# Four scan sweeps of a convolution layer: VectorE kept in the text's order, and the statistics of a column block taken eight steps behind its sum

## The chip, the cores and the metric

The kernel runs on one core of a Trainium2 chip. The metric is the device time of one execution in microseconds; a kernel's time is the median of its runs.

## What is computed

The input is an image of 48 channels and 128 x 128 pixels in fp32. Four layers follow one another. Each normalises its input in groups of channels, passes it through a block and adds the result to the input:

```
x = x + attention(_gn(x))       # layer 0
x = x + sweeps(_gn(x))          # layer 1
x = x + patch convolution(_gn(x))   # layer 2
x = x + state space scan(_gn(x))    # layer 3
```

`_gn` subtracts the mean of a group of three channels over the whole image and divides by its standard deviation. So a layer can't begin to normalise before the last pixel of the layer ahead of it is summed and counted.

The layer of this case is layer 1. It goes over the image line by line, and each line is its input plus a convolution (five taps, 48 channels to 48, with a bias) of the line before:

```
def step(w, b):
    def f(carry, inp):
        nxt = inp + _conv1d(carry, w, b)
        return (nxt, nxt)
    return f
```

There are four such sweeps, each over the result of the one before: down the rows, up the rows, to the right over the columns, and to the left over the columns. Every step needs the result of the step before it.

## The kernel before

`tile_kernel` calls `attention`, `sweeps`, `patch_conv`, `image_out` and `scan` in turn. Two large buffers in SBUF, `xa` and `xb`, each 128 partitions high, hold the image. In `sweeps` (L553 to L688) `other` is `xb` and `xq` is `xa`. The rows of the image lie in `t`, a view of `xb`, for the first two sweeps, and its columns in `u`, a view of `xa`, for the last two.

`steps` (L618 to L626) lists 508 steps, 127 for each sweep; step n computes one line. `down`, `up` and `right` (L627) are 127, 254 and 381 and mark the ends of the first, second and third sweep. So the left sweep begins at n = 381, and step n of it computes column 507 - n.

One step of the loop (L654) is this. Three matmuls (L656) on TensorE add the convolution of the line before into the PSUM tile `p`, which `begin` (L632) has already started with the input line and the bias. `begin` for the next step is written behind them. Then VectorE multiplies `p` with `mask` into the new line (L664). That line is the operand of the next step's matmuls, so the matmuls and the multiply follow one another in a ring. While the up sweep runs, `turn` copies its rows into columns on ScalarE (L640).

While the left sweep runs, the residual sum is made as well. `sums` (L643 to L645) divides the columns into blocks: seven of 16 columns, then 8, 4 and 4 at the end. At the step that computes a block's leftmost column (n = 395 for x = 112, and then every 16 steps up to n = 491 for x = 16, and 499, 503 and 507 for x = 8, 4 and 0), GpSimd adds the block of `u` to the layer's input, which has been loaded into `xb` (L672, L677). Each block is then cut into pieces of 512 elements, four for a block of 16 columns, two for the block of 8 and one for each of the last two, and put into the list `todo` (L683). `stretch` (L648) takes a piece from the list and runs `bn_stats` on it on VectorE (L650), which leaves its mean and variance in `st`. There are 32 pieces. The text calls `stretch` at every third step if more than four pieces wait (L684), and for the rest after the loop (L687).

At the beginning of the next layer, `group_stats` (L71) puts the 32 results together, and the layer's normalisation (L93) waits for it. The borders that this layer sets on GpSimd (L747, L760) and its loads of weights (L103, L105, L713 and the following lines) are written after the sweeps in the text.

The order of the instructions on each engine is not that of the text. The kernel is written in a tile framework, whose scheduler orders the instructions of an engine by its own estimate of when each can begin, and sets the semaphores. Where the order is to be kept, the kernel uses the class `InOrder` (L38 to L60). It stands in for an engine and ties each instruction that it issues to the one issued before it, so that the scheduler can't exchange the two; the tie sets no semaphore. `attend`, for example, issues through it on ScalarE and TensorE (L310). In `sweeps` VectorE's instructions are not tied.

Of the kernel before, what the change touches and what calls it, by code (L numbers as in the profile page):

```python
# [27 lines left out]
H = W = 128  # L28
# [37 lines left out]
def group_stats(nc, pool, psum, const, name="gn_ps"):  # L66


    st, gmat = const["st"], const["gmat"]
    mv = pool.tile([C, 2], F32, name="gn_mv")  # L70
    nc.vector.bn_aggr(mv, st)  # L71
    pm = psum.tile([C, 1], F32, name=name)
    nc.tensor.matmul(pm, lhsT=gmat, rhs=mv[:, 0:1], start=True, stop=True)
    mean = pool.tile([C, 1], F32, name="gn_mean")
    nc.vector.tensor_copy(mean, pm)

    dev = pool.tile([C, 1], F32, name="gn_dev")
    nc.vector.tensor_sub(dev, mv[:, 0:1], mean)
    var = pool.tile([C, 1], F32, name="gn_var")
    nc.vector.scalar_tensor_tensor(var, dev, dev, mv[:, 1:2], ALU.mult, ALU.add)  # L80
    pv = psum.tile([C, 1], F32, name=name)
    nc.tensor.matmul(pv, lhsT=gmat, rhs=var, start=True, stop=True)
    std = pool.tile([C, 1], F32, name="gn_std")
    nc.vector.tensor_scalar_add(std, pv, 1e-5)  # L84
    nc.scalar.activation(std, std, AF.Sqrt)  # L85
    rstd = pool.tile([C, 1], F32, name="gn_rstd")
    nc.vector.reciprocal(rstd, std)
    return mean, rstd
# [7 lines left out]
def rows(ap, n=W):  # L96
    return ap.rearrange("c (r w) -> c r w", w=n)
# [455 lines left out]
@with_exitstack  # L553
def sweeps(ctx, tc, xq, other, x1, const, ins):

    nc = tc.nc
    pool = ctx.enter_context(tc.tile_pool(name="l1", bufs=1))
    ps1 = ctx.enter_context(tc.tile_pool(name="l1_ps1", bufs=1, space=PSUM))
    ps = ctx.enter_context(tc.tile_pool(name="l1_ps", bufs=2, space=PSUM))
    K = 64 + C
    E = 3
    S = W + 2 * E
    L = W + 1


    w = pool.tile([128, 3, 3, K], F32, name="w")
    nc.sync.dma_start(w, ins["l1_w"])
    wi = pool.tile([128, 3, K], F32, name="wi")
    nc.sync.dma_start(wi, ins["l1_wi"])
    mask = pool.tile([128, L], F32, name="mask")
    nc.gpsimd.memset(mask, 1.0)
    nc.gpsimd.memset(mask[0:C, 0:1], 0.0)
    nc.gpsimd.memset(mask[64:128, W : W + 1], 0.0)


    t = other[:, 0 : S * S].rearrange("c (h s) -> c h s", s=S)
    u = xq[:, 0 : W * S].rearrange("c (w s) -> c w s", s=S)
    low, high = slice(0, E - 1), slice(S - E, S)

    def borders(b, lines):

        inside = slice(E - 1, E + W)
        nc.gpsimd.memset(b[32:64, lines, inside], 1.0)
        for pad in (low, high):  # L590
            nc.gpsimd.memset(b[:, lines, pad], 0.0)
        nc.gpsimd.memset(b[0:C, lines, E - 1 : E], 0.0)
        nc.gpsimd.memset(b[64:K, lines, E + W - 1 : E + W], 0.0)  # L593

    borders(t, slice(E, E + H))
    mean, rstd = group_stats(nc, pool, ps1, const)
    off = pool.tile([C, 1], F32, name="off")
    nc.vector.scalar_tensor_tensor(off, mean, -1.0, rstd, ALU.mult, ALU.mult)
    RN = 8
    for r in range(0, H, RN):  # L600
        for at, x in ((0, E), (64, E - 1)):
            nc.scalar.activation(
                t[at : at + C, E + r : E + r + RN, x : x + W],
                rows(xq[0:C, r * W : (r + RN) * W]),
                AF.Identity,
                bias=off,
                scale=rstd,
            )

    borders(u, slice(0, W))  # L610

    def row(h):
        return t[:, E + h, :]

    def col(x):
        return u[:, x, :]

    steps = []  # L618
    for h in range(1, H):
        steps.append((0, row(h), row(h), row(h - 1)))  # L620
    for h in range(H - 2, -1, -1):
        steps.append((0, row(h), row((h - 1) % H), row(h + 1)))
    for x in range(1, W):
        steps.append((1, col(x), col(x), col(x - 1)))
    for x in range(W - 2, -1, -1):
        steps.append((2, col(x), col(x), col(x + 1)))  # L626
    down, up, right = H - 1, 2 * (H - 1), 3 * (H - 1)  # L627

    def begin(n):
        which, _, inp, _ = steps[n]  # L630
        p = ps.tile([K, L], F32, name="p")
        nc.tensor.matmul(  # L632
            p, lhsT=wi[0:K, which, :], rhs=inp[0:K, E - 1 : E + W], start=True, stop=False
        )
        return p

    def turn(h):

        for at, y in ((0, E + h), (64, E + h - 1)):
            nc.scalar.copy(u[at : at + C, :, y], t[0:C, E + h, E : E + W])  # L640


    sums = {}  # L643
    for x, width in [(x, 16) for x in range(16, W, 16)] + [(8, 8), (4, 4), (0, 4)]:
        sums[x] = rows(other[0:C, 0:N])[:, :, x : x + width]  # L645
    todo, done = [], []

    def stretch():  # L648
        xr = todo.pop(0)
        nc.vector.bn_stats(const["st"][:, len(done), :], xr)  # L650
        done.append(xr)

    p = begin(0)
    for n, (which, out, inp, state) in enumerate(steps):  # L654
        for i in range(3):
            nc.tensor.matmul(  # L656
                p,
                lhsT=w[0:K, which, i, :],
                rhs=state[0:K, 2 * i : 2 * i + L],
                start=False,  # L660
                stop=(i == 2),
            )
        nxt = begin(n + 1) if n + 1 < len(steps) and n + 1 != up else None
        nc.vector.tensor_mul(out[0:K, E - 1 : E + W], p, mask[0:K])  # L664
        if n == down:
            turn(H - 1)
        if down <= n < up:
            turn(H - 2 - (n - down))
        if n + 1 == up:

            for r in range(0, N, 2048):
                nc.sync.dma_start(other[0:C, r : r + 2048], x1[:, r : r + 2048])  # L672
            nxt = begin(up)
        x = 4 * (H - 1) - 1 - n
        if n >= right and x in sums:
            xr = sums[x]
            nc.gpsimd.tensor_add(  # L677
                xr,
                xr,
                u[0:C, x : x + xr.shape[2], E : E + H].rearrange("c w h -> c h w"),  # L680
            )
            step = CH // xr.shape[2]
            todo += [xr[:, r : r + step] for r in range(0, H, step)]  # L683
        if n % 3 == 0 and len(todo) > 4:  # L684
            stretch()
        p = nxt
    while todo:  # L687
        stretch()  # L688
# [800 lines left out]
@with_exitstack  # L1489
def tile_kernel(ctx: ExitStack, tc: tile.TileContext, ins: dict, out: bass.AP):  # L1490
    nc = tc.nc
    cp = ctx.enter_context(tc.tile_pool(name="const", bufs=1))
    dram = ctx.enter_context(tc.tile_pool(name="x3", bufs=1, space=bass.MemoryType.DRAM))
    const = constants_on_chip(tc, cp, ins)
    x1 = dram.tile([C, N], F32, name="x1")
    x3 = dram.tile([C, N], F32, name="x3")
    with ExitStack() as image:
        xp = image.enter_context(tc.tile_pool(name="image", bufs=1))

        xa = xp.tile([128, W * (W + 6)], F32, name="xa")  # L1500
        xb = xp.tile([128, (H + 6) * (W + 6)], F32, name="xb")
        for i in range(0, N, 2048):
            nc.sync.dma_start(xa[0:C, i : i + 2048], ins["x"][:, i : i + 2048])
        attention(tc, xa, xb, x1, const, ins)
        sweeps(tc, xa, xb, x1, const, ins)
        patch_conv(tc, xb, xa, const, ins)
        image_out(tc, xb, x3, const)
    scan(tc, x3, const, ins, out)
# [189 lines left out]
```

## Time and profile before

| | |
|---|---|
| time before, median of 3 runs | 7754.8 us (7753.7 to 7766.08) |
| profiled execution, span | 7757.9 us |
| PE, ACT, DVE and POOL busy | 81%, 57%, 44%, 36% of the span |
| L664, the multiply of a step | 508, 291 to 295 ns each for most |
| L650, statistics of a piece | 32, 676 ns each |
| L677, GpSimd's sum, seven of 48 x 2048 | 5.5 us each |
| L677, one of 48 x 1024 and two of 48 x 512 | 2.81 us, 1.48 and 1.50 us |
| first and last multiply of the rows' two sweeps | 3844.1 and 4177.4 us |
| first and last multiply of the columns' two sweeps | 4180.8 and 4565.1 us |

PE is TensorE, DVE is VectorE, ACT is ScalarE and POOL is GpSimd. All starts are microseconds from the span's start. A line of the timeline gives the start, the duration, the engine, the line of the kernel, the operation, what is written and read, and in brackets how long the engine was idle before it and whose result ended that. "x6" says that six instructions are merged in one line. PEclk is the clock that TensorE was granted, as a share of the full one. Each fp32 matmul of the text is carried out as several instructions, so TensorE's counts are larger than those of the text.

### The profile page before, as it was taken

What the parts mean: (1) busy time and instruction counts of PE and PEld (TensorE: products, weight loads), DVE (VectorE), ACT (ScalarE), POOL (GpSimd) and SP (SyncE); (2) the same over time, 40 slices, a digit from 0 to 9 for tenths busy, and PEclk for the clock granted to TensorE, in tenths of its full rate; (3) what the DMA queues carried; (4) which work ended last, traced back from release to release, by engine and by line L of the source; (5) the groups of instructions that cost most, each with busy time, mean ns of one, the idle gap of its engine ahead of it and who ended that gap; (6) DMA issues with size and microseconds to landing.
All of it is one profiled execution on the core that took longest, in us unless ns stands there. A gap on an engine that the chain in (4) does not pass through costs nothing. (4 is left out here: it accounts for less than half of the span.)

```text
span 7757.9 us, 203399 instructions
## 1 busy us (share of the span) xinstructions
PE 6262.9 (81%) x93872; PEld 3179.6 (41%) x93872; DVE 3376.3 (44%) x2467; ACT 4458.0 (57%) x4928; POOL 2793.1 (36%) x573
## 2 busy tenths in 40 slices
PE   7999999999999999999888879845545554554555
PEld 2333333333333333333377655434334343434444
DVE  8300000000000000000122224489999999999998
ACT  2566666666666666666623014366666666666665
POOL 1000000000000000000100112279999999999998
PEclk9999999999999999999999989866766766776666
DMA  5000000000000000000000001156556566666776
GB/s 75 11 2 3 3 2 3 3 3 2 3 3 3 2 3 3 3 2 3 6 5 13 1 27 50 25 150 166 158 160 164 151 162 156 165 156 159 182 179 148
DMA packets 167598, 488.84 MB, mean 63 GB/s; under 512 B 33441, under 2 KB 51969, under 8 KB 163985
## 3 DMA queue, kind: packets, MB, share of 16 engines
q1 hardware_dynamic: 160704, 470.30, 24.2%
q8 instruction: 737, 12.08, 0.7%
q10 hardware_dynamic: 6032, 5.44, 0.3%
q14 instruction: 125, 1.02, 0.0%
HBM read 428.86 MB, written 22.02 MB: 58 GB/s over the span
## 5 line engine op out<-in xcount | busy, mean ns | idle before, releaser
L48 ACT ACTIVATE e<-s,absT 128x1024 f32<-128x1024 f32 x2048 | 2279.3, 1115 | 1215.1 <-PE s L48 1215.1
L1458 POOL TENSOR_TENSOR h<-du,bt 128x3072 f32<-128x3072 f32 (+1 forms) x386 | 2559.8, 6681 | 100.9 <-DMA du<-rep 73.0
L48 PE MATMUL s<-xa,xb 49*64 49x512 f32 x16384 | 2124.3, 589 | 10.6 <-DVE xb L266 10.6
L48 PE MATMUL acc<-e,xb 64*64 64x512 f32 x16384 | 2120.3, 588 | 0.0
L1465 DVE TENSOR_TENSOR_SCAN h<-dA,carry,h 128x1024 f32<-128x1024 f32 x864 | 1940.1, 2323 | 48.1 <-ACT dA L48 31.9
L48 ACT ACTIVATE dA<-dt,a 128x1024 f32<-128x1024 f32 x1152 | 1287.2, 1118 | 866.5 <-DVE h L1465 855.6
L48 PE MATMUL y<-h,cw 128*32 128x48 f32 x49152 | 908.6, 247 | 950.5 <-issue 504.4
L361 DVE TENSOR_TENSOR osum<-o 128x512 f32<-128x512 f32 x32 | 22.1, 692 | 3114.0 <-ACT o L48 3114.0
L593 POOL MEMSET xa<- 48x128 f32 x1 | 0.3, 328 | 3560.2 <-PE acc L48 3560.2
L48 PEld LDWEIGHTS y<-h,cw 128*32 128x32 f32 x49152 | 818.3, 141 | 1072.3 <-issue 656.6
L48 PEld LDWEIGHTS s<-xa,xb 49*64 49x64 f32 x16384 | 618.1, 132 | 1158.8 <-issue 607.2
L48 PEld LDWEIGHTS acc<-e,xb 64*64 64x64 f32 x16384 | 620.4, 132 | 1141.6 <-issue 1118.9
L1465 DVE TENSOR_TENSOR_SCAN h<-dA,h 128x1024 f32<-128x1024 f32 x288 | 636.1, 2270 | 45.6 <-ACT dA L48 34.8
L48 PE MATMUL yz<-ev,sel 128*8 128x48 f32 x4096 | 193.0, 259 | 273.0 <-ACT ev L48 270.2
L656 PE MATMUL p<-xa,w 112*112 112x129 f32 x1524 | 258.4, 310 | 66.4 <-DVE xa L664 66.1
L48 PEld LDWEIGHTS yz<-ev,sel 128*8 128x8 f32 x4096 | 162.5, 106 | 331.1 <-ACT ev L48 301.2
L656 PE MATMUL p<-xb,w 112*112 112x129 f32 x1524 | 236.5, 291 | 41.8 <-DVE xb L664 41.7
L677 POOL TENSOR_TENSOR xb<-xb,xa 48x2048 f32<-48x2048 f32 (+2 forms) x10 | 44.3, 4430 | 618.8 <-DVE xa L664 618.8
L656 PEld LDWEIGHTS p<-xa,w 112*112 112x112 f32 x1524 | 202.6, 194 | 120.4 <-DVE xa L664 120.4
L85 ACT ACTIVATE gn_std<-gn_std 48x1 f32<-48x1 f32 x4 | 0.8, 203 | 425.3 <-DVE gn_std L84 419.0
L656 PEld LDWEIGHTS p<-xb,w 112*112 112x112 f32 x1524 | 184.3, 179 | 93.7 <-DVE xb L664 93.7
L640 ACT COPY xa<-xb 48x128 f32<-48x128 f32 x256 | 107.4, 420 | 197.2 <-issue 138.8
(187 smaller groups left out, 3719.3 us busy)
## 6 DMA issues: line engine op xcount, KB each, us to landing
du<-rep SPq DMA_DIRECT2D x768, 256.0 KB
dt<-rep SPq DMA_DIRECT2D x768, 256.0 KB
rest<-xa SPq DMA_DIRECT2D x96, 77.0 KB
rest<-band SPq DMA_DIRECT2D x48, 129.9 KB
rep<-dd SPq DMA_DIRECT2D x24, 192.0 KB
yd<-ys ACTq DMA_DIRECT2D x256, 12.0 KB
band<-band SPq DMA_DIRECT2D x8, 414.4 KB
xa<-xa SPq DMA_DIRECT2D x16, 199.1 KB
```

What stands on the lines that cost most here:

```text
L48: ins = method(*args, **kwargs).ins
L85: nc.scalar.activation(std, std, AF.Sqrt)
L361: nc.vector.tensor_add(self.o, o[:, 0], o[:, 1])
L593: nc.gpsimd.memset(b[64:K, lines, E + W - 1 : E + W], 0.0)
L640: nc.scalar.copy(u[at : at + C, :, y], t[0:C, E + h, E : E + W])
L656: nc.tensor.matmul(p, lhsT=w[0:K, which, i, :], rhs=state[0:K, 2 * i : 2 * i + L], start=False, stop=(i == 2),)
L677: nc.gpsimd.tensor_add(xr, xr, u[0:C, x : x + xr.shape[2], E : E + H].rearrange("c w h -> c h w"),)
L1458: nc.gpsimd.tensor_mul(h[:, p, ks], du.unsqueeze(1).to_broadcast([128, ks.stop - ks.start, LC]), r["bt"][:, ks],)
L1465: nc.vector.tensor_tensor_scan(h[:, p, k, :], dA, h[:, p, k, :], carry[:, i, k : k + 1] if ci else 0.0, ALU.mult, ALU.add,)
```

## The change

VectorE's instructions of the sweeps, that is the multiplies and the statistics, are issued through an `InOrder`, so that they keep the order of the text. A piece enters the list with the step from which it may be taken, eight after the step that issued the sum of its block. A step takes one piece, if the first of the list is due, and does so behind its multiply; the rule of every third step with more than four waiting is gone. What is left after the loop is taken there, as before. The statistics of a piece keep their places in `st`.

```diff
     todo, done = [], []
+    dve = InOrder(tc, nc.vector)
 
     def stretch():
-        xr = todo.pop(0)
-        nc.vector.bn_stats(const["st"][:, len(done), :], xr)
+        _, xr = todo.pop(0)
+        dve.bn_stats(const["st"][:, len(done), :], xr)
         done.append(xr)
...
-        nc.vector.tensor_mul(out[0:K, E - 1 : E + W], p, mask[0:K])
+        dve.tensor_mul(out[0:K, E - 1 : E + W], p, mask[0:K])
...
             step = CH // xr.shape[2]
-            todo += [xr[:, r : r + step] for r in range(0, H, step)]
-        if n % 3 == 0 and len(todo) > 4:
+            todo += [(n + 8, xr[:, r : r + step]) for r in range(0, H, step)]
+        if todo and n >= todo[0][0]:
             stretch()
```

## The prediction

> **What bounds the kernel now.** I read the page first: PE 81%, ACT 57%, DVE 44% and POOL 36% busy over the span, so nothing is full everywhere and the answer lies in a stage. The chain that ended last names only the final stage (L1465, L1458) and does not reach back to the sweeps, so I went to the busy times by stretch of time, of the end of the third sweep and of the stretch in which the sums and their statistics are made:
>
> ```profile
> core 0: us, PE busy (x) PEld busy (x) DVE busy (x) ACT busy (x) POOL busy (x), PEclk, DMA share, GB/s
> 4180.00:4365.00 185.00, 161.68 (x1134) 132.69 (x1134) 41.59 (x142) 0.00 (x0) 0.04 (x1) 0.99 0.01 2
> 4365.00:4565.00 200.00, 156.89 (x894) 131.70 (x894) 50.87 (x142) 0.00 (x0) 57.00 (x25) 0.81 0.00 1
> ```
>
> Both stretches run the same loop. The first has 142 VectorE instructions in 185 us and a TensorE clock of 0.99; the second has 142 in 200 us, but 31 of those are statistics, so fewer steps got done, at a clock of 0.81. The waits by source line, between 4364 and 4566 us, say on whom VectorE waits (busy us and mean ns; then idle before):
>
> ```profile
> L664 DVE TENSOR_TENSOR xa<-p,mask 112x129 f32<-112x129 f32 x113 | 32.9, 291 | 116.4 <-PE p L656 116.4
> L650 DVE BATCH_NORM_STATS2 st<-xb 48x6 f32<-48x512 f32 x31 | 20.4, 676 | 34.0 <-POOL xb L677 34.0
> ```
>
> The second line is the point: VectorE stands idle 34.0 us for GpSimd's sum (L677) in front of L650. The timeline shows one such place (start, duration, then the idle time before and its releaser):
>
> ```profile
> 4364.96 5.49 POOL L677 TENSOR_TENSOR xb<-xb,xa 48x2048 f32<-48x2048 f32 x1 [475.87 <-DVE xa L664]
> 4365.83 0.29 DVE L664 TENSOR_TENSOR xa<-p,mask 112x129 f32<-112x129 f32 x1 [1.01 <-PE p L656]
> 4366.18 0.92 PE L656 MATMUL p<-xa,w 112*112 112x129 f32 x6 [0.17 <-DVE xa L664]
> ...
> 4370.49 0.69 DVE L650 BATCH_NORM_STATS2 st<-xb 48x6 f32<-48x512 f32 x1 [4.36 <-POOL xb L677]
> ...
> 4371.10 0.27 DVE L664 TENSOR_TENSOR xa<-p,mask 112x129 f32<-112x129 f32 x1
> 4371.29 1.27 DVE L650 BATCH_NORM_STATS2 st<-xb 48x6 f32<-48x512 f32 x2
> ...
> 4371.42 1.63 PE L656 MATMUL p<-xa,w 112*112 112x129 f32 x6 [4.10 <-DVE xa L664]
> ```
>
> A step is a closed ring: three products on TensorE, the multiply L664 on VectorE, and TensorE again. One step takes 1.299 us (138 steps between the multiplies at 4185.27 and 4364.53 us). At 4367.1 the matmuls are done and the next multiply could go; but VectorE's queue has a statistics instruction ahead of it, which starts only at 4370.49, when the sum is over. So the multiply comes at 4371.10, 5.27 us after the last. In the program's text this L650 stands at n = 411 at the earliest, fourteen steps later (L684 asks for more than four waiting pieces, and a block brings four): the framework's scheduler has pulled it forward. And TensorE, idle 4.10 us, then takes 1.63 us for the burst that took 0.92. The stretch ends on this ring; what follows (L71, then the next layer) needs the last statistics, and so inherits every microsecond.
>
> [...] full clock for the 138 steps, whose TensorE gaps are below 0.4 us; after the 4.10 us gap come steps of about 2.01 us. [...] L664 reads one operand from PSUM; the multiply at 4365.83, inside a sum, took 0.29 like all others. [...]
>
> **The change part by part.**
>
> *Statistics no longer ahead of the multiplies.* I split the loss from the sum of block x=112 (multiply n=395, at 4364.53) to the last multiply (n=507, at 4565.13): 112 steps in 200.60 us. At 1.299 they would take 145.5; the loss is 55.1 us. Direct waits: the nine intervals between multiplies that hold a wait are 5.27, 5.29, 5.29, 5.30, 5.28, 5.28, 5.29 (the seven wide blocks), 3.19 (x=8) and 2.58 (x=4). Less 1.30 each, that is 27.9 + 1.9 + 1.3 = 31.1 us. The rest, 24.0 us, are 34 slow steps behind these waits at about 2.01 instead of 1.30 (34 x 0.71 = 24.1). The two agree with the total.
>
> *Is the sum there eight steps later?* Eight steps are 10.4 us. A sum starts 0.43 us after its multiply's start and takes 5.5, so it is over at 5.9 us: 4.5 us to spare. Blocks are sixteen steps apart (20.8 us) and their four pieces leave at steps 8 to 11, so nothing piles up. The nearest case, x=16 (n=491, pieces at 499 to 502) before x=8 (n=499, due 507), also fits. GpSimd's other work there is the border memsets of the next layer (L760, 0.94 us each), pulled into its idle time; those on columns still to be added stand behind the sum anyway, and two take 1.83 us, within the margin. So all direct waits go, and with them the gaps that slow the clock: minus 55.1 us.
>
> *One statistics instruction inside a step.* It now follows the multiply. In the trace such a one starts 0.19 us after the multiply's start (4371.29 after 4371.10) and ends about 0.88 after it; the next multiply is due at 1.30. It fits with 0.42 us to spare in VectorE's idle 1.01 us. The step from 4373.09 to 4375.10, with one inside, took 2.01, like slow steps without. It also overlaps no sum except at the end. I cost it at 0; the upper bound, all 29 statistics inside the loop at their full 0.68, is 19.7 us, the lower 0, as it only adds work.
>
> *The end.* Now three pieces (the second of x=8, x=4, x=0) and the one that falls at n=507 follow the last multiply. Four at 0.60 us apart (4371.29, 1.27 us for two) from 0.20 us on: the last starts at 2.0 us. Before, it waited for the last sum and started at 1.88 (4567.01 less 4565.13). Plus 0.1 us, between 0 and 0.6.
>
> *Not moved:* instruction counts, DMAs and their queues (SP's x1 loads L672 ran in the second sweep), GpSimd's sums, and the first 395 steps. The setup loads of the next layer are issued at 4565.45, right behind the last multiply, so they move forward with it. The next layer fills TensorE (100.00 of 100 us busy from 4700 to 4900) and the last is held by VectorE and GpSimd (98.30 and 100.00 of 100 in 5100 to 5200): both run just as long, earlier. One small unknown is the clock at entry: 14 matmuls at 4576.11 took 6.40 us, 12 at 4600.78 took 3.18. If warm, they would save up to 2.7 us, but the matmuls behind them, which read copies issued from 4574.38 on, start only at 4586.90; I take 0.
>
> Sum: -55.1 + 0.1 = **-55.0 us**. On the profiled execution's span of 7757.9 that is 7702.9; the three runs lie at 7753.7 to 7766.08, and off their median of 7754.8 it gives **7699.8 us**.
>
> **The rivals.**
>
> *The statistics don't hide in the step.* For it: VectorE has one more instruction per step, on its critical ring. Against: 0.42 us of slack. Time: 7699.8 + 19.7 = 7719.5. Chance 0.05.
>
> *The change doesn't do what it says, or gives the gain back later:* the scheduler puts the statistics elsewhere, or the next layer waits for something that doesn't move. For it: the scheduler already overruled the text. Against: the order is tied instruction to instruction, and the next layer's loads hang on the last multiply. Time: 7755. Chance 0.04.
>
> *Slower: the clock falls and stays down.* Mechanism: with statistics between the multiplies the TensorE gaps grow and the half clock, today on 34 of 112 steps, holds for nearly all. At 2.015 instead of 1.299, all 112 cost 80.2 us, against 55.1 of loss today: 25 us slower, 7780. It decides from 55.1 / 0.716 = 77 slow steps on. For it: slow runs after one wait lasted up to six steps without more waits. Against: 138 steps in a row at 0.99 with the same gaps. Chance 0.03.
>
> **How the numbers follow.** Forecast 0.88, rivals 0.05, 0.04, 0.03. The range reaches down to 7690 (the warm entry, 2.7, the lowest run, 1.1 below the median[...]) and up to 7720 (the statistics not hidden; the highest of the three runs, 11.3 above the median, lies within). A measurement can tell about 0.2%, 15.5 us, from no change. Forecast and first rival are faster: 0.93; same 0.04; slower 0.03.
>
> **What would show it.** In the changed profile: no idle time of DVE L650 for POOL L677 except at most at the last; multiplies 1.30 us apart from x=112 to the end, 29 of the 32 statistics each right behind a multiply; clock near 1.0 in place of 0.81; the last multiply 145.5 us after n=395; next layer as long as before. Wrong if steps with statistics are longer than 1.30, if slow steps stay without waits, or if the next layer starts 55 us earlier and ends less so.

## The result, and the profile after

The changed kernel takes 7700.5 us (median of 4 runs, 7695.29 to 7707.8); the kernel before, run beside it, takes 7756.2 (4 runs). The ratio is 0.9927, with a 95% interval of 0.9909 to 0.9944: 0.7% faster, and clear of the 0.2% that a measurement can tell. The forecast was 7699.8.

The busy times by stretch of time, of the changed kernel, show the right sweep with the first steps of the left one, and then the time of the sums (columns as before):

```profile
4180.00:4365.00 185.00, 161.36 (x1129) 132.85 (x1130) 41.02 (x140) 0.39 (x1) 0.00 (x0) 0.99 0.01 3
4365.00:4512.00 147.00, 128.32 (x906) 105.14 (x904) 49.67 (x141) 0.00 (x0) 57.34 (x25) 1.00 0.00 1
```

The second stretch now takes 147 us for nearly the VectorE work (141 instructions, 49.67 us) that took 200 us before, and its clock is 1.00 instead of 0.81. GpSimd's work in it, 57.34 us, is nearly the same (57.00).

The groups of instructions between 4364 and 4520 us show who waits. The statistics and the multiplies now have the line of the helper, L48, so they are told apart by their tiles:

```profile
L678 POOL TENSOR_TENSOR xb<-xb,xa 48x2048 f32<-48x2048 f32 (+2 forms) x10 | 44.6, 4464 | 563.0 <-DVE xa L48 563.0
L48 DVE TENSOR_TENSOR xa<-p,mask 112x129 f32<-112x129 f32 x115 | 33.7, 293 | 99.2 <-PE p L657 99.2
L48 DVE BATCH_NORM_STATS2 st<-xb 48x6 f32<-48x512 f32 x32 | 21.4, 675 | 0.0
```

In the last line stands 0.0 where 34.0 us of waiting for GpSimd stood. The timeline shows the first block, whose multiply n = 395 began at 4366.46 (start, duration, and in brackets the idle time before):

```profile
4366.88 5.54 POOL L678 TENSOR_TENSOR xb<-xb,xa 48x2048 f32<-48x2048 f32 x1 [475.40 <-DVE xa L48]
...
4376.86 0.29 DVE L48 TENSOR_TENSOR xa<-p,mask 112x129 f32<-112x129 f32 x1 [1.01 <-PE p L657]
4377.06 0.68 DVE L48 BATCH_NORM_STATS2 st<-xb 48x6 f32<-48x512 f32 x1
4377.20 0.92 PE L657 MATMUL p<-xa,w 112*112 112x129 f32 x6 [0.16 <-DVE xa L48]
4378.15 0.29 DVE L48 TENSOR_TENSOR xa<-p,mask 112x129 f32<-112x129 f32 x1 [0.41 <-PE p L657]
4378.36 0.68 DVE L48 BATCH_NORM_STATS2 st<-xb 48x6 f32<-48x512 f32 x1
```

The sum is over at 4372.42. Its first piece is taken at 4377.06, 4.6 us later, with no wait in front of it. The next multiply comes 1.29 us after the last, and VectorE even then idles 0.41 us for TensorE instead of 1.01: the statistics lie inside the idle time. The burst stays at 0.92 us. From n = 395 to the last multiply (4512.01) it is 145.55 us, and every step in between takes 1.30. This stretch is called "the stretch" below; it was 200.60 us in the kernel before.

At the end of the sweep four statistics follow the last multiply, one of them taken at the last step:

```profile
4512.01 0.29 DVE L48 TENSOR_TENSOR xa<-p,mask 112x129 f32<-112x129 f32 x1 [1.01 <-PE p L657]
4512.22 2.45 DVE L48 BATCH_NORM_STATS2 st<-xb 48x6 f32<-48x512 f32 x4
...
4512.38 1.50 POOL L678 TENSOR_TENSOR xb<-xb,xa 48x512 f32<-48x512 f32 x1 [3.62 <-DVE xa L48]
...
4514.70 1.01 DVE L71 BATCH_NORM_AGGREGATE gn_mv<-st 48x2 f32<-48x192 f32 x1
```

L71 begins 2.69 us after the last multiply, against 2.60 (4567.73 less 4565.13) before.

Of the profiled spans, 7757.9 and 7706.0, the difference is 51.9 us: the stretch gave 55.05, the end took 0.09, the multiply n = 395 came 1.93 later in this execution, and from L71 to the end it took 1.1 more. The last two lie in parts that the change doesn't touch.

### The profile page after: what moved, and what is told of

It is laid out like the page before. It is cut to its first block, busy times and chain, and to the rows that moved or that the text cites. A ratio compares the mean times of both kernels' runs of the same rounds, so it can differ in the third digit from the quotient of the medians.

```text
span 7706.0 us, 203399 instructions
## 1 busy us (share of the span) xinstructions
PE 6227.8 (81%) x93872; PEld 3159.4 (41%) x93872; DVE 3377.0 (44%) x2467; ACT 4455.4 (58%) x4928; POOL 2793.0 (36%) x573
## 5 line engine op out<-in xcount | busy, mean ns | idle before, releaser
L48 ACT ACTIVATE e<-s,absT 128x1024 f32<-128x1024 f32 x2048 | 2277.3, 1114 | 1217.9 <-PE s L48 1217.9
L48 PE MATMUL s<-xa,xb 49*64 49x512 f32 x16384 | 2128.4, 589 | 10.6 <-DVE xb L266 10.6
L48 PE MATMUL acc<-e,xb 64*64 64x512 f32 x16384 | 2125.0, 588 | 0.0
L48 ACT ACTIVATE dA<-dt,a 128x1024 f32<-128x1024 f32 x1152 | 1287.2, 1118 | 864.0 <-DVE h L1466 854.5
L48 PE MATMUL y<-h,cw 128*32 128x48 f32 x49152 | 899.2, 246 | 949.0 <-issue 511.9
L48 PEld LDWEIGHTS y<-h,cw 128*32 128x32 f32 x49152 | 809.9, 140 | 1072.3 <-issue 661.8
L48 PEld LDWEIGHTS s<-xa,xb 49*64 49x64 f32 x16384 | 626.3, 132 | 1151.2 <-issue 615.6
L48 PEld LDWEIGHTS acc<-e,xb 64*64 64x64 f32 x16384 | 628.6, 132 | 1133.7 <-issue 1111.2
L48 PE MATMUL yz<-ev,sel 128*8 128x48 f32 x4096 | 192.9, 260 | 277.2 <-ACT ev L48 273.3
L48 PEld LDWEIGHTS yz<-ev,sel 128*8 128x8 f32 x4096 | 162.5, 106 | 334.9 <-ACT ev L48 308.7
L657 PE MATMUL p<-xa,w 112*112 112x129 f32 x1524 | 233.5, 289 | 41.8 <-DVE xa L48 41.8
L678 POOL TENSOR_TENSOR xb<-xb,xa 48x2048 f32<-48x2048 f32 (+2 forms) x10 | 44.6, 4464 | 563.0 <-DVE xa L48 563.0
L657 PEld LDWEIGHTS p<-xa,w 112*112 112x112 f32 x1524 | 181.8, 177 | 93.3 <-DVE xa L48 93.3
L369 DVE RECIPROCAL rec<-y 48x512 f32<-48x512 f32 x32 | 107.1, 3348 | 257.5 <-ACT y L48 257.5
```

Source lines behind the costliest of these rows:

```text
L48: ins = method(*args, **kwargs).ins
L369: nc.vector.reciprocal(rec, y[64 : 64 + C])
L657: nc.tensor.matmul(p, lhsT=w[0:K, which, i, :], rhs=state[0:K, 2 * i : 2 * i + L], start=False, stop=(i == 2),)
L678: nc.gpsimd.tensor_add(xr, xr, u[0:C, x : x + xr.shape[2], E : E + H].rearrange("c w h -> c h w"),)
```

## The experiments

The stretch is read off the profile of each kernel, as the time from the multiply of n = 395 to the last one. "Median" is the time of the whole kernel; those with one run are marked. A single run's time also holds differences from other parts of the kernel: with four steps, layer 3 alone took 8.6 us longer than in the profile of the changed kernel. So the stretch is what to compare.

| kernel | median, us | kernel before beside it | stretch, us |
|---|---|---|---|
| before | | 7756.2 | 200.60 |
| changed | 7700.5 | 7756.2 | 145.55 |
| tie alone, old rule | 7704.1 | 7752.2 | 145.52 |
| eight-step rule alone | 7755.1 | 7752.2 | 201.44 |
| one step behind the sum | 7749.0 | 7752.2 | 199.34 |
| two steps | 7738.5 (one run) | 7758.6 | 182.76 |
| three steps | 7723.9 (one run) | 7758.6 | 167.44 |
| three steps, again | 7720.6 (one run) | 7756.8 | 159.17 |
| four steps | 7717.8 (one run) | 7758.6 | 146.22 |
| all statistics after the loop | 7715.6 | 7752.2 | 145.52 |
| each statistics twice | 7717.1 (one run) | 7756.8 | 151.40 |
| each three times | 7752.8 (one run) | 7758.6 | 191.71 |

### Which of the two parts does it

The tie alone, with the old rule:

```diff
-        if todo and n >= todo[0][0]:
+        if n % 3 == 0 and len(todo) > 4:
             stretch()
```

> VectorE is tied to the text's order, but the old rule decides when a piece is taken (every third step with more than four waiting), so the first piece of a block comes sixteen steps behind its sum. Theory (the order is what counts, and any distance over 5.9 us will do): no wait of a statistics instruction for GpSimd's sum inside the loop, 145.5 us from the multiply of n = 395 to the last one, clock near 1.0, seven statistics left behind the last multiply instead of four, 1.8 us more at the end; so 53 us below the kernel before. Rival (the eight-step rule is needed, or statistics that now overlap a sum get in its way): waits or longer steps stay, and less than 45 us are gained.

Measured: a stretch of 145.52 us, a ratio to the kernel before of 0.9935 (0.9918 to 0.9952). L71 begins 4.48 us after the last multiply instead of 2.69, so the seven statistics left over cost 1.8 us more, as expected. The statistics that now run beside a sum got in nobody's way: one at 4385.18 took 0.68 us, and the sum that began under it at 4385.41 took 5.55.

The eight-step rule alone:

```diff
-    dve = InOrder(tc, nc.vector)
+    dve = nc.vector
```

> The eight-step rule without the tie: the scheduler may move the statistics. Theory: it pulls them forward as before, the same nine waits stand, 200.6 us from the multiply of n = 395 to the last, same time as before within 0.2%. Rival (the place in the text decides): 145.5 us there, and 55 us below the kernel before.

Measured: a stretch of 201.44 us and a ratio of 1.0002 (0.9993 to 1.0011). The timeline of this kernel shows the first statistics again ahead of the multiply of n = 397 (the third line), although the text puts it behind that of n = 403:

```profile
4361.40 0.29 DVE L665 TENSOR_TENSOR xa<-p,mask 112x129 f32<-112x129 f32 x1 [1.01 <-PE p L657]
4366.06 0.69 DVE L651 BATCH_NORM_STATS2 st<-xb 48x6 f32<-48x512 f32 x1 [4.37 <-POOL xb L678]
4366.67 0.27 DVE L665 TENSOR_TENSOR xa<-p,mask 112x129 f32<-112x129 f32 x1
4366.86 1.27 DVE L651 BATCH_NORM_STATS2 st<-xb 48x6 f32<-48x512 f32 x2
```

So the tie carries the gain. The rule of eight steps alone does nothing, since the scheduler overrules it; under the tie it is worth the 1.8 us at the end.

### Is it the wait for the sum

The tie kept, the distance cut from eight steps to one, two, three and four:

```diff
-            todo += [(n + 8, xr[:, r : r + step]) for r in range(0, H, step)]
+            todo += [(n + 1, xr[:, r : r + step]) for r in range(0, H, step)]
```

> The tie kept, but a piece may be taken one step behind its sum. Theory (the wait for the sum is the cost, whoever puts the instruction there): the first piece of each wide block again waits until 5.9 us after the sum's multiply, so seven intervals of 5.3 us, the clock falls again behind each; 195 to 203 us from n = 395 to the last multiply, same time as before within 8 us. Rival (the tie itself, or one piece per step, is the gain): 145.5 us, 55 us below before.

> A piece may be taken two steps behind its sum. The first piece of a wide block then stands behind the multiply at 2.60 us and waits until about 5.96; the next multiply comes at 6.57 instead of 3.90. Theory (direct wait and clock are two costs): 7 x 2.67 = 18.7 us of direct waits, and a TensorE gap of 3.0 us. If a gap of that length leaves the clock alone, 164.2 us from n = 395 to the last multiply; if it lowers it as the gap of 4.1 us did, some 24 us more, 188. Rival (all of the loss scales with the wait): 55.1 x 18.7 / 31.1 = 33 us of loss, 178.6 us.

> Three steps behind the sum: the first piece stands behind the multiply at 3.90 us, the next multiply comes at 6.57 instead of 5.20, so 7 x 1.37 = 9.6 us of direct waits and TensorE gaps of 1.7 us. Theory (a short gap leaves the clock alone): no slow steps, 155.1 us from n = 395 to the last multiply. Rival (all of the loss scales with the wait): 17 us of loss, 162.5 us.

> Four steps behind the sum: the first piece waits about 0.5 us, but has a slack of 0.42 in its step, so 7 x 0.1 us at most are lost. Theory: 145.5 to 146.3 us from n = 395 to the last multiply, the whole gain. Rival (eight steps are needed): several us more.

With one step the loss is back, tie or no tie: 199.34 us, the ratio 0.9994 (0.9985 to 1.0003). The groups between 4355 and 4566 us of this kernel:

```profile
L48 DVE BATCH_NORM_STATS2 st<-xb 48x6 f32<-48x512 f32 x32 | 21.7, 678 | 34.4 <-POOL xb L678 34.4
```

34.4 us of waiting before the 32 statistics, against 35.6 before the 32 of the kernel before (34.0 for the 31 that ran up to 4566 us). So the position relative to the sum is the cause, and the tie is only the means.

The direct waits came as worked out: the steps that hold one lasted 4.0 us with a distance of two (7 x 2.69 = 18.8 us over the normal step), 2.72 with three (9.9 us) and 1.42 with four (0.8 us). But what is left over besides, the clock's part, was not as I thought. With two steps it is 182.76 - 145.5 - 18.8 = 18.5 us, between my two cases: slow steps of 2.01 to 2.02 us follow all seven waits. The bursts behind the first take 1.63 us instead of 0.92, as in the slow steps of the kernel before, where the granted clock was 0.50 (4398.29 to 4403.95 us). With three it is 167.44 - 145.5 - 9.9 = 12.0 us, where I had expected none. In both the stretch lies nearer to the rival (178.6 and 162.5) than to my own figures. But the clock's part isn't in proportion to the wait, as the rival has it: it is 0.77 of the direct part in the kernel before, 0.98 with two steps, 1.2 with three, and nothing with four. With three steps slow bursts come after a gap of 1.55 us already, here behind the sum of n = 411 (timeline of TensorE):

```profile
4388.66 0.38 PE L632 MATMUL p<-xa,wi 112*112 112x129 f32 x2
4390.60 0.96 PE L657 MATMUL p<-xa,w 112*112 112x129 f32 x6 [1.55 <-DVE xa L48]
4391.36 0.64 PE L632 MATMUL p<-xa,wi 112*112 112x129 f32 x2
4391.95 1.63 PE L657 MATMUL p<-xa,w 112*112 112x129 f32 x6
```

The burst after the gap still takes 0.96 us, the next one 1.63. In the block before, a gap of 1.54 us was followed by bursts of 0.91 and 0.92 us. To see whether the place decides, I ran the same kernel once more:

> The kernel of three steps' distance once more, unchanged. There the gap of 1.54 us lowered the clock behind five of the seven wide blocks and not behind the other two. Theory[...]: other blocks this time, four to seven of them, the sum of direct waits again 9.9 us. Rival (the place in the kernel decides): the blocks of n = 395 and 427 are spared again.

This time slow steps stood behind the blocks of n = 411 and 427 only, two of seven, and the stretch was 159.17 us (13.7 us over 145.5, of which 9.9 are direct). In the first run the blocks of 395 and 427 were the ones spared. So neither the place in the kernel nor the number of four to seven that I gave holds. Why one of two equal gaps is followed by slow steps and the other not is not shown.

### Are the statistics hidden in their step

All of them moved behind the loop:

```diff
-            todo += [(n + 8, xr[:, r : r + step]) for r in range(0, H, step)]
+            todo += [(n + 200, xr[:, r : r + step]) for r in range(0, H, step)]
```

> The tie kept, all 32 statistics behind the loop. Theory (inside a step they are hidden): 145.5 us from n = 395 to the last multiply, as in the changed kernel; behind it 32 statistics 0.60 us apart, the last starting 18.8 us after the last multiply instead of 2.0, so 16.8 us slower than the changed kernel and 38 us below before. Rival (inside a step they lengthen it by up to 0.68 us): the loop gets shorter by up to 20 us, and the time is that of the changed kernel or a little less.

Measured: 145.52 us, against 145.55 with 29 of them inside. They cost nothing there. The end shows what they cost in the open:

```profile
4508.79 0.29 DVE L48 TENSOR_TENSOR xa<-p,mask 112x129 f32<-112x129 f32 x1 [1.01 <-PE p L657]
4509.00 19.05 DVE L48 BATCH_NORM_STATS2 st<-xb 48x6 f32<-48x512 f32 x32
4527.98 1.33 DVE L106 TENSOR_TENSOR wt<-wt,w 128x1152 f32<-128x1152 f32 x1
4529.24 1.00 DVE L71 BATCH_NORM_AGGREGATE gn_mv<-st 48x2 f32<-48x192 f32 x1
```

L71 begins 20.45 us after the last multiply, 17.8 more than in the changed kernel: 16.6 from the statistics (19.05 less 2.45), the rest from L106, which stands ahead of L71 here. The ratio to before is 0.9949 (0.9933 to 0.9966).

The other way round, more of them in a step, two or three with the same operands and the same place in `st`:

```diff
-        dve.bn_stats(const["st"][:, len(done), :], xr)
+        for _ in range(3):
+            dve.bn_stats(const["st"][:, len(done), :], xr)
```

> The changed kernel with each statistics instruction issued three times, to the same place. Theory (a step has 0.42 us of room behind one of them): three start at 0.20, 0.80 and 1.40 us after the multiply and the next multiply comes at 2.0 instead of 1.30; 28 such steps, 20 us more from n = 395 to the last multiply, 165 us, and 4.8 us more at the end. Rival (VectorE has room to spare, or the two added ones run beside something else): under 150 us. If the longer TensorE gaps of 1.1 us lowered the clock, steps would be longer than 2.0 us or slow steps would follow.

> Each statistics instruction issued twice, to the same place. With three of them the step took 2.23 us and the clock fell after four such steps, whose TensorE gap is 1.09 us. With two the step should take 1.54 us (one of 0.71 less, less what is no longer waited for) and the gap be 0.4 us. Theory[...]: the clock stays, no slow steps, 28 x 0.24 = 6.7 us more than 145.5 from n = 395 to the last multiply. Rival (any step longer than normal lowers it): slow steps behind each group, 165 us or more.

With two, a step takes 1.51 to 1.53 us, and the stretch is 151.40 us, 5.9 over 145.5; no slow steps. With three, a step takes 2.23 instead of the 2.0 I expected, because equal ones follow 0.71 us apart (2.12 us for three) and not 0.60; at the end L71 begins 7.2 us later than in the changed kernel instead of 4.8. And slow steps follow (timeline of VectorE with three; the burst at 4380.57 takes 1.63 us, those before it 0.91 and 0.92):

```profile
4378.02 0.27 DVE L48 TENSOR_TENSOR xa<-p,mask 112x129 f32<-112x129 f32 x1
4378.21 2.11 DVE L48 BATCH_NORM_STATS2 st<-xb 48x6 f32<-48x512 f32 x3
4380.25 0.27 DVE L48 TENSOR_TENSOR xa<-p,mask 112x129 f32<-112x129 f32 x1
4382.24 0.29 DVE L48 TENSOR_TENSOR xa<-p,mask 112x129 f32<-112x129 f32 x1 [1.73 <-PE p L658]
4384.26 0.29 DVE L48 TENSOR_TENSOR xa<-p,mask 112x129 f32<-112x129 f32 x1 [1.73 <-PE p L658]
```

The last two lines are steps without any statistics, and they take 1.99 and 2.02 us. The stretch is 191.71 us: 28 steps with 0.93 us too much make 26.0, and the rest, 20.2, comes from slow steps. So most of the gain is gone again without one wait for GpSimd.

## Why the prediction was right

- **The wait that bounds the stretch.** The prediction put the loss of 55.1 us down to statistics that the scheduler had pulled ahead of the multiplies. Shown: the tie alone takes the loss away, the distance alone doesn't, and the tie with a distance of one step brings it back.
- **The sum of the loss.** Forecast 145.5 us for the stretch, measured 145.55. That the time of the whole kernel came within 0.7 us of the forecast is in part luck: the four runs lie up to 12 us apart, and between the two profiled executions the gain is 51.9 us. The nine waits and all slow steps are gone. The split, 31.1 us of direct waits and 24.0 of slow steps, holds as well: with one step's distance the direct part is 29.3 (seven intervals of 5.3 and one of 2.61, less 1.30 each) and the rest is 24.5.
- **Is the sum there eight steps later.** Forecast 4.5 us to spare before the piece's step; measured 4.6 to the piece itself. The sums took 5.53 to 5.55 us where they had taken 5.49 to 5.51: 0.04 us, of no weight. The statistics aren't the reason, since with all of them behind the loop the ten sums take 4461 ns on average, as in the changed kernel (4464; before 4430); what the reason is, is not shown. Four steps would do, with 0.7 us lost in the stretch.
- **Statistics at no cost.** Forecast 0 with a bound of 19.7; measured 0.03 us between all and none of them inside. The slack of 0.42 us was 0.41.
- **The end.** Forecast plus 0.1, measured 0.09.
- **Work after it.** Layer 2, from L71 to the next L71, took 446.79 us before and 446.81 after, with a granted clock of 0.73 before and 0.76 after in its first 52.3 us. Over all these kernels it lies between 446.5 and 447.9. Nothing was given back there. Layer 3 ranges from 2739 to 2753 us with no order that follows the change.
- **The rivals.** Statistics that don't hide, and a change that does nothing, are excluded for this kernel. That the clock stays down didn't happen at one piece per step, with no slow step where 77 were needed and a granted clock of 1.00; with three pieces per step slow steps did come, and cost 20.2 us.

What didn't hold is a side of the reasoning about the clock. The prediction went by gaps below 0.4 us, with a granted clock of 0.99, and by a gap of 4.10 us, with steps of about 2.01 us after it. That a short gap leaves the clock alone, as the expectation for three steps says of 1.7 us, was the author's estimate. But the profile before already has a place that speaks against it. Behind the wait for the sum of x = 8 TensorE stood idle for 2.03 us only, and the second burst after it was slow all the same:

```profile
4553.55 0.92 PE L656 MATMUL p<-xa,w 112*112 112x129 f32 x6 [2.03 <-DVE xa L664]
4554.85 1.63 PE L656 MATMUL p<-xa,w 112*112 112x129 f32 x6
```

In the experiments slow steps followed the seven waits with two steps' distance every time (gap 2.82 us at the first), those with three sometimes (1.55 us), and the groups of three statistics per step every time (gaps of 1.09 to 1.10 us in a row). This changed no number of the forecast, since all gaps vanished, but it gave the wrong expectation for two and three steps.

## What to carry to other kernels

In a ring of two engines, a foreign instruction that is cheap in itself (0.68 us) costs what it waits for: look which instruction stands ahead of the ring's own in the queue and for whom it waits, and count the clock's fall behind the gap as well, here 24 of 55 us. A place in the text isn't a place in the queue where a scheduler orders it; tie the order first, then choose the distance longer than the producer's time. Before putting work into a ring's idle time, compare its duration with the slack: one piece left 0.41 us to spare, two cost 0.2 us a step, and behind three came slow steps of 2.0 us.

## What the runs showed of the hardware that wasn't expected

In these runs no long idle time of TensorE was needed for slow steps. With three statistics per step TensorE is busy 1.13 of 2.23 us, in gaps of 1.09 us, and slow steps of 1.99 to 2.02 us follow four such steps in all seven blocks. With two it is busy 1.13 of 1.51 us, in gaps of 0.37, and no slow step follows in any of the seven. With a distance of three steps the waiting step lasts 2.70 to 2.73 us, with a gap of 1.54 and 1.55 us behind the first two blocks of the first run, and slow steps followed behind five of seven blocks in that run and two of seven in the other. With two steps (a gap of 2.82 us behind the first block) they followed behind all seven, and with four (0.26 us) behind none. What tells equal gaps apart, and what ends the slow steps, is not shown.

Equal statistics to one place follow 0.71 us apart, different ones 0.60 (19.05 us for 32); whether the shared place or the shared source causes that wasn't tried.
